# Regrouping a local unit's four feed-forward output runs in a two-layer transformer kernel

## The chip, the core and the metric

The kernel runs on one core of one Trainium2 chip, as one launch. The metric is the time of one execution on the device, in microseconds, as the median of several executions. A profiled execution gives, beside its own time, a span from its first to its last instruction and a trace of every engine: TensorE (PE, with its weight loads as PEld), VectorE (DVE), ScalarE (ACT), GpSimd (POOL) and SyncE (SP, which here only issues DMAs).

## The reference, cut to what matters

```python
x = L0_attn_X                                            # 8 sequences x 512 tokens x 256
x = x + L0_attn(layernorm(x));  x = x + L0_experts(layernorm(x))
x = x + L1_attn(layernorm(x));  x = x + L1_local(layernorm(x))

def L1_local(x):                                         # two layers of this:
    for l in range(2):
        q, k, v = split(shift_token(x) @ wqkv[l])        # 8 heads of 64
        q, k = rotary_xpos(l2norm(q) * qs[l], l2norm(k) * ks[l])
        o = softmax over the own and the previous window of 128 tokens
        x = x + o @ wo[l]
        h = layernorm(shift_token(x)) * lg[l] + lb[l]
        a, g = split(h @ w1[l] + b1[l])                  # 682 wide each
        x = x + (a * gelu(g)) @ w2[l] + b2[l]
    return x
```

The change concerns the last line of the local layers, `(a * gelu(g)) @ w2 + b2`, and the q and k columns of `h @ wqkv` of the unit that comes after. Everything is float32.

## The kernel before, in words

The program runs four stages: attention, the experts (up to 575 us), attention of 16 heads (597 to 1174 us), and the local layers (to the end, 2553 us, their first products lying among the last work of the stage before). A local **unit** is one layer of one sequence of 512 tokens; there are 16 units, in four blocks of 128 tokens each (`t` = 0 to 3).

The loop at L1581 is a pipeline written out by hand. Iteration n works on four units at once: `u` = unit n (attention, block by block), `ahead` = unit n+1 (its projections, later its rotations), `late` = unit n-1 (its norm and the first feed-forward product, "gated"), and `last` = unit n-2 (the second feed-forward product, "back"). The attention of block t is emitted in the order `flip_weights(t)` (the transposes `pt`), `outputs(t)` (`ov`), `scores(t+1)` (`sc`), `exponentials(t+1)`, `project(t)` (`pr`), `weigh(t+1)`. The table `fill` says what of the three other units stands between: `fill[t][0]` between the transposes and `ov`, `fill[t][1]` between `ov` and the scores, `fill[t][2]` after `pr`. The `weigh` of a quad of heads is emitted after the first and after the second step of `fill[t][2]`.

What the steps around the change do:

- `back(t)` (L1102): 6 float32 products of 256 columns, which the trace shows as 12 matmuls `fo`; five have 128 rows of weights, the last has 43 (42 hidden rows and the bias). VectorE then adds the result to the residual (L1122).
- `rows(t, s)` (L865), s = 0 for q and 1 for k: the products `qp` (4 matmuls of 512 columns), ScalarE's square `sq` (L870), VectorE's products with the rotary tables (L872, and L877 twice) and the sum of squares (L886), GpSimd's sum (L885).
- `flip()` (L840): the transposes `tp` of the next unit's rows, copied by ScalarE (L851).
- `norm()` (L1025): statistics (L1030 to L1032), the root on ScalarE (L114), then eight VectorE instructions that write `hn` (L1039). Half of a normed row is the row of the token before; for this `project(t)` (L1005) sends the rows through two DMAs into `late` (L1021, L1023) after its sum (L1018).
- `flip_normed()` (L1048): the transposes `tp` of `hn`, and VectorE's scale and shift into `hT`, a half at a time (L1058). `gated(i)` (L1067), the next consumer, multiplies with both halves of `hT` (`fp`).
- `masked_largest` (L148, called at L934): eight VectorE instructions on the scores of a block, which ScalarE's eight exponentials wait for.

What sets the order. Every product and every transpose of these stages goes through `product` and `transpose` (L161, L165), which pin it behind the instruction traced before it on its engine, so TensorE's order is the code's. So are ScalarE's exponentials, table loads and roots: a root is pinned behind the ScalarE instruction emitted just before it. The other instructions of VectorE, ScalarE and GpSimd are ordered by the framework's planner at build time, from its own estimates of when their inputs are ready. At run time each engine's queue keeps that order.

All of `fo`, `qp`, `tp`, `tpq` and `fp` take their PSUM tile from the pool `ps` (L1130), which has three slots, in turn. `pt` and `sc` share two slots of `psb`; `ov` and `pr` share the one of `psa`.

Of the kernel before, what the change touches and what calls it, by code (L numbers as in the profile page):

```python
# [53 lines left out]
def forward_kernel(  # L54
# [140 lines left out]
    with ExitStack() as st:  # L195
# [289 lines left out]
        for b in range(B):  # L485
            keep = tc.keep_in_program_order
            for t in range(NT):
# [9 lines left out]
                last = (b, t - 1) if t else (b - 1, NT - 1)  # L497
# [45 lines left out]
    with ExitStack() as st:  # L543
# [8 lines left out]
        number, steps = slots[0:1, :NS], slots[:, NS : NS + 32]  # L552
# [160 lines left out]
        ahead = None  # L713
        for s in range(NS):
# [4 lines left out]
            ahead = (s, hT, g, c2, r)  # L719
# [22 lines left out]
    def load_qkv(l, pool):  # L742
        wqkv = pool.tile([P, NC, 3 * INNER], F32, name=f"wqkv2_{l}")
        later(nc.sync.dma_start(out=wqkv, in_=wqkv2[l].rearrange("(c p) o -> p c o", p=P)))
        return wqkv

    def load_layer(l):
        wo = wl.tile([P, INNER // P, D], F32, tag="wo2", name=f"wo2_{l}")
        later(nc.sync.dma_start(out=wo, in_=wo2[l].rearrange("(c p) o -> p c o", p=P)))
        wf1 = wl.tile([P, NC, 2 * FULL + GATE + LAST], F32, tag="wf1", name=f"wf1_{l}")  # L750
        later(nc.sync.dma_start(out=wf1, in_=w1[l].rearrange("(c p) o -> p c o", p=P)))

        wf2 = wl.tile([P, NFC, D], F32, tag="wf2", name=f"wf2_{l}")
        for dst, src in (
            (wf2[:, : NFC - 1, :], w2[l, :FULL, :].rearrange("(c p) o -> p c o", p=P)),
            (wf2[:LAST, NFC - 1, :], w2[l, FULL:, :]),
            (wf2[LAST : LAST + 1, NFC - 1, :], b2[l : l + 1, :]),
        ):
            later(nc.sync.dma_start(out=dst, in_=src))
        return wo, wf1, wf2  # L760
# [375 lines left out]
    with ExitStack() as st:  # L1136
# [379 lines left out]
        for slot in range(max(max(fill) + 1, END + 3)):  # L1516
            steps = []
# [25 lines left out]
    with ExitStack() as st:  # L1543
        d1 = st.enter_context(tc.tile_pool(name="pD1", bufs=1))
        d2 = st.enter_context(tc.tile_pool(name="pD2", bufs=2))
        psb = st.enter_context(tc.tile_pool(name="psDb", bufs=2, space=PSUM))
        psa = st.enter_context(tc.tile_pool(name="psDa", bufs=1, space=PSUM))

        wqkv_of.append(load_qkv(1, d1))

        uT = d1.tile([P, NFC, L], F32, name="uT")
        nc.vector.memset(uT[:, NFC - 1, :], 1.0)
        lates = [d1.tile([P, NT, P], F32, name=f"late{i}") for i in range(2)]
        for late in lates:
            nc.gpsimd.memset(late[0:1, 0, :], 0.0)

        qT = d1.tile([P, H2 // 2, L], F32, name="qT")
        kT = d1.tile([P, H2 // 2, L], F32, name="kT")

        def unit(n):  # L1560
            return units[n] if 0 <= n < len(units) else None

        def steps(u, *names):

            return [(getattr(u, name), args) for name, *args in names] if u else []

        u = units[0]
        for t in range(NT):
            u.turn(t)
            if t == 0:  # L1570
                for quad in range(2):
                    u.scores(0, quad)
                for quad in range(2):
                    u.exponentials(0, quad)
        for quad in range(2):
            u.weigh(0, quad)

        for n in range(len(units) + 2):  # L1581
            u, ahead, late, last = unit(n), unit(n + 1), unit(n - 1), unit(n - 2)
            fill = [
                [
                    steps(last, ("back", 0)),
                    steps(late, ("norm",)) + steps(last, ("back", 1)) + steps(ahead, ("flip",)),
                    steps(last, ("back", 2))
                    + steps(ahead, ("rows", 0, 0))
                    + steps(last, ("back", 3))
                    + steps(ahead, ("rows", 0, 1))  # L1590
                    + steps(late, ("flip_normed",)),
                ],
                [
                    steps(late, ("gated", 0), ("gated", 1)),
                    steps(ahead, ("value_rows", 0)),
                    steps(ahead, ("rows", 1, 0), ("rows", 1, 1), ("rows", 2, 0)),
                ],
                [
                    steps(late, ("gated", 2), ("gated", 3)),
                    [],  # L1600
                    steps(ahead, ("rows", 2, 1), ("rows", 3, 0), ("rows", 3, 1)),
                ],
                [
                    steps(ahead, ("roots",)) + steps(late, ("gated", 4), ("gated", 5)),
                    steps(ahead, *(("turn", t) for t in range(NT))),
                    steps(ahead, *(("value_rows", t) for t in range(1, NT))),
                ],
            ]
            for t in range(NT):
                then, at = (u, t + 1) if t + 1 < NT else (ahead, 0)  # L1610
                if u:
                    u.flip_weights(t)
                for do, args in fill[t][0]:
                    do(*args)
                if u:
                    u.outputs(t)
                for do, args in fill[t][1]:
                    do(*args)
                if then:
                    for quad in range(2):  # L1620
                        then.scores(at, quad)
                    for quad in range(2):
                        then.exponentials(at, quad)
                if u:
                    u.project(t)
                rest = fill[t][2]
                for i, (do, args) in enumerate(rest):
                    do(*args)
                    if i < 2 and then:
                        then.weigh(at, i)  # L1630
                if then:
                    for i in range(len(rest), 2):
                        then.weigh(at, i)
            if u and u.b == B - 1 and u.l + 1 < DEPTH:
                layers.append(load_layer(u.l + 1))
# [146 lines left out]
```

## Time and profile before

| | |
|---|---|
| runs (3) | median 2559.63 us, 2558.3 to 2562.59 |
| the profiled execution | 2554.89 us, of which its span is 2553.2 us |
| granted TensorE clock | 0.987 over the span; 1.00 in the local layers |
| 0 to 560 us | PE busy 518.09, DVE 253.83, ACT 116.25 |
| 560 to 1240 us | PE busy 628.27, DVE 449.58, ACT 319.23 |
| 1240 us to the end | PE busy 1293.15, DVE 847.03, ACT 686.98, POOL 162.22 |
| one iteration of the loop (1413.37 to 1498.88 us) | 85.51 us: PE busy 85.18, DVE 56.93, ACT 45.97, POOL 10.21 |

The iterations that have all four units (n = 2 to 14, 13 of them) begin 85.50 to 85.52 us apart, so one iteration can be read for all. Times below that are given "in the iteration" count from the start of its first `pt` run, which in the one shown is at 1413.37 us. A run is a stretch of TensorE matmuls of one kind; in a row of the timeline the second number is the time from the first start to the modelled end of the last, and the difference between the starts of two rows is what a run really takes up.

### The profile page before, as it was taken

The page shows a single profiled execution, that of the slowest core. Times are in us where ns is not written, and L with a number is a line of the kernel's source. Part 1 is how long each engine was busy: PE and PEld are TensorE (multiplying, and loading weights), DVE is VectorE, ACT ScalarE, POOL GpSimd, SP SyncE. Part 2 cuts the span into 40 slices and gives each one's busy share as a digit, 9 for nine tenths or more (in the row PEclk, how much of TensorE's full clock was granted, in tenths as well). Part 3 has the DMA queues.
Part 4 walks back from the last instruction along what each step waited for, and adds up shares of the span by engine and source line. Part 5 has one row for each costly group of instructions (what it writes and reads, how often), then busy time and mean ns, then how long its engine had stood idle before and what let it go on. Part 6 is the DMA issues. An engine that isn't in the chain of part 4 may idle for free.

```text
span 2553.2 us, 39603 instructions
## 1 busy us (share of the span) xinstructions
PE 2439.5 (96%) x14374; PEld 1560.1 (61%) x14374; DVE 1550.4 (61%) x4739; ACT 1122.5 (44%) x2504; POOL 471.0 (18%) x642
## 2 busy tenths in 40 slices
PE   8998699996999999998899999999999999999998
PEld 5666588883455555445566666666666666666565
DVE  6775322224667777666667566756676667666653
ACT  2222121112455555545465455555555555555552
POOL 2232101003333332231111011100111111111100
PEclk9999899997999999999999999999999999999999
DMA  5340666631012000001000000000000000000000
GB/s 172 102 144 34 202 230 229 206 132 54 9 35 74 14 12 12 9 11 52 4 4 4 4 4 4 4 4 4 12 8 33 20 4 21 20 21 4 20 21 27
DMA packets 79030, 126.45 MB, mean 50 GB/s; under 512 B 13406, under 2 KB 56820, under 8 KB 78580
## 3 DMA queue, kind: packets, MB, share of 16 engines
q1 hardware_dynamic: 73236, 109.37, 12.9%
q0 software_dynamic: 4096, 12.59, 1.4%
q8 instruction: 115, 1.88, 0.3%
q10 hardware_dynamic: 1504, 1.97, 0.2%
q14 instruction: 79, 0.65, 0.1%
HBM read 97.82 MB, written 29.10 MB: 50 GB/s over the span
## 4 chain that ended last, share of the span: by engine, by line
PE 67%; DVE 6%; ACT 2%; DMA 1%; issue 1%; POOL 0%; SPq 0%; DVEq 0%; POOLq 0%; ACTq 0%
PE qp L163 12%; PE fp L163 12%; PE fo L163 7%; PE sc L163 7%; PE ov L163 7%; PE sd L163 5%; PE pr L163 5%; PE tpq L166 4%; PE pt L166 3%; PE qk L163 2%; DVE scrap L150 1%; PE tp L166 1%; PE vp L163 1%; DVE hT L1058 1%; DVE turn L877 1%; ACT prob L944 1%
## 5 line engine op out<-in xcount | busy, mean ns | idle before, releaser
L885 POOL TENSOR_TENSOR turned<-turned,turn 128x512 f32<-128x512 f32 x128 | 163.4, 1276 | 1060.1 <-DVE turn L877 1019.4
L163 PE MATMUL qp<-wqkv,xT 128*128 128x512 f32 x768 | 350.7, 598 | 0.0
L150 DVE CUSTOM_DVE_ANT_0 scrap<-sc,masks 128x256 f32<-128x256 f32 (+1 forms) x500 | 243.1, 486 | 134.3 <-PE sc L163 118.7
L163 PE MATMUL fp<-hT,wf 128*128 128x512 f32 (+1 forms) x704 | 313.5, 595 | 5.8 <-DVE hT L1058 5.7
L163 PE MATMUL sc<-kT,qT 64*128 64x256 f32 (+2 forms) x2024 | 305.3, 420 | 9.4 <-DVE qrow L150 7.7
L150 DVE CUSTOM_DVE_ANT_0 prob<-sc,masks 128x256 f32<-128x256 f32 (+1 forms) x512 | 164.4, 387 | 147.9 <-PE sc L163 147.9
L1326 ACT ACTIVATE pT<-sd 128x768 f32<-128x768 f32 (+1 forms) x192 | 169.3, 882 | 182.8 <-PE sc L163 92.6
L944 ACT ACTIVATE prob<-prob,nmax 128x256 f32<-128x256 f32 (+1 forms) x512 | 239.1, 468 | 22.5 <-DVE nmax L150 21.9
L163 PEld LDWEIGHTS qp<-wqkv,xT 128*128 128x128 f32 x768 | 141.6, 190 | 152.1 <-issue 134.4
L163 PEld LDWEIGHTS fp<-hT,wf 128*128 128x128 f32 (+1 forms) x704 | 127.9, 188 | 158.3 <-issue 138.9
L163 PE MATMUL sd<-qA,kT 32*128 32x512 f32 (+3 forms) x1024 | 194.4, 474 | 11.1 <-ACT pT L1326 9.0
L163 PEld LDWEIGHTS sc<-kT,qT 32*128 32x128 f32 (+1 forms) x2024 | 167.8, 187 | 59.3 <-DVE qrow L150 27.8
L163 PE MATMUL fo<-wf,uT 128*128 128x256 f32 (+1 forms) x768 | 190.4, 390 | 0.0
L690 DVE TENSOR_SCALAR hT<-hp,c 128x128 f32<-128x128 f32 x156 | 54.4, 349 | 211.7 <-ACT hT L688 211.7
L688 ACT ACTIVATE hT<-hp,c 128x128 f32<-128x128 f32 x156 | 57.4, 368 | 259.6 <-PE hp L678 221.3
L163 PEld LDWEIGHTS fo<-wf,uT 128*128 128x128 f32 (+1 forms) x768 | 137.6, 189 | 46.7 <-issue 29.6
L678 PEld LDWEIGHTS hp<-gT,we 128*128 128x128 f32 x1248 | 148.3, 193 | 26.1 <-DVE hT L690 14.1
L678 PE MATMUL hp<-gT,we 128*128 128x128 f32 x1248 | 159.8, 282 | 3.3 <-DVE krow L1164 1.6
L870 ACT ACTIVATE sq<-qp 128x512 f32<-128x512 f32 x128 | 75.8, 593 | 178.7 <-PE qp L163 135.7
L701 PE MATMUL yp<-w_all,hT 128*128 x624 | 153.7, 380 | 0.6 <-ACT hT L688 0.6
L1328 POOL TENSOR_SCALAR_AFFINE_SELECT pT<-pT 128x256 f32<-128x256 f32 x256 | 101.8, 411 | 277.8 <-ACT pT L1326 277.7
L1098 DVE SCALAR_TENSOR_TENSOR uT<-fp,b_sb,ge 128x512 f32<-128x512 f32 x96 | 69.9, 740 | 124.0 <-PE fp L163 119.2
(223 smaller groups left out, 4098.5 us busy)
## 6 DMA issues: line engine op xcount, KB each, us to landing
we<-in_ew SPq DMA_DIRECT2D x39, 1024.0 KB
g<-rows_in SPq DMA_DIRECT2D x39, 256.0 KB
w_all<-in_ew SPq DMA_DIRECT2D x8, 1024.0 KB
rows_out<-in_c_zero SPq DMA_DIRECT2D x3, 1664.0 KB
c<-in_eb SPq DMA_DIRECT2D x39, 128.0 KB
rows_out<-y SPq DMA_DIRECT2D x39, 128.0 KB
xb<-in_x_in SPq DMA_DIRECT2D x8, 512.0 KB
kept<-x SPq DMA_DIRECT2D x8, 512.0 KB
```

What stands on the lines that cost most here:

```text
L150: nc.vector.tensor_tensor_reduce(out=out, in0=scores, in1=mask, scale=-1.0, scalar=-MASKED, op0=ALU.add, op1=ALU.min, accum_out=largest,)
L163: tc.keep_in_program_order(nc.tensor.matmul(*args, **kw))
L166: tc.keep_in_program_order(nc.tensor.transpose(dst, src, ident))
L678: nc.tensor.matmul(hp[:, f, :], we[:, c, f * P : (f + 1) * P], gT[:, c, :], start=(c == 0), stop=(c == NC - 1),)
L688: nc.scalar.activation(hT[:, f, :], hp[:, f, :], AF.Relu, bias=bias)
L701: nc.tensor.matmul(yp, hT[:, f, :], w2_all[:, bass.ds(e, 1), f * D : (f + 1) * D].rearrange("p a d -> p (a d)"), start=(f == 0), stop=(f = ...
L870: nc.scalar.activation(sq, qp, AF.Square)
L885: nc.gpsimd.tensor_tensor(own.turned[:, t, s], own.turned[:, t, s], turn, ALU.add)
L944: nc.scalar.activation(pr[:, j, lo:], pr[:, j, lo:], AF.Exp, scale=-1.0, bias=nmax[:, j : j + 1], accum_out=sums[:, j : j + 1],)
L1098: nc.vector.scalar_tensor_tensor(uT[:n, i, :], val[:n, :], b1_sb[:n, l, 0, i : i + 1], ge[:n, :], ALU.add, ALU.mult)
L1326: nc.scalar.activation(pT[:, :, :at], sc[:, :, :at], AF.Exp)
L1328: nc.gpsimd.affine_select(out=pT[:, :, a : a + P], in_=pT[:, :, a : a + P], compare_op=ALU.is_ge, fill=0.0, base=0, pattern=[[0, 2], [1, P ...
```

## The change

The list `fill[0]` is rewritten. All steps are kept; only their order within block 0 changes, and with it the order in which everything of theirs is emitted.

```diff
             fill = [
                 [
-                    steps(last, ("back", 0)),
-                    steps(late, ("norm",)) + steps(last, ("back", 1)) + steps(ahead, ("flip",)),
-                    steps(last, ("back", 2))
-                    + steps(ahead, ("rows", 0, 0))
-                    + steps(last, ("back", 3))
-                    + steps(ahead, ("rows", 0, 1))
+                    steps(last, ("back", 0), ("back", 1)),
+                    steps(late, ("norm",)) + steps(ahead, ("flip",)),
+                    steps(last, ("back", 2), ("back", 3))
+                    + steps(ahead, ("rows", 0, 0), ("rows", 0, 1))
                     + steps(late, ("flip_normed",)),
                 ],
```

On TensorE, block 0 before: `pt`, back 0, `ov`, back 1, `tp` (flip), `sc`, `pr`, back 2, rows 0 q, back 3, rows 0 k, `tp` (normed). After: `pt`, back 0, back 1, `ov`, `tp` (flip), `sc`, `pr`, back 2, back 3, rows 0 q, rows 0 k, `tp` (normed). The `weigh` of the first quad is still emitted behind back 2; that of the second stands behind back 3 instead of behind rows 0 q.

## The prediction

> **What bounds the kernel.** I read the page first, then the waits from 1327.86 us on (the iterations with all four units), then TensorE's and VectorE's timelines of one iteration, then the end of the trace. The page says who fills the span:
>
> ```profile
> span 2553.2 us, 39603 instructions
> PE 2439.5 (96%) x14374; PEld 1560.1 (61%) x14374; DVE 1550.4 (61%) x4739; ACT 1122.5 (44%) x2504; POOL 471.0 (18%) x642
> PEclk9999899997999999999999999999999999999999
> ```
>
> TensorE is full, and in the local layers at a granted clock of 1.00. An iteration is 85.51 us with PE busy 85.18, so the change can act in two ways only: on what TensorE's own runs take up, and on the few places where it waits. VectorE's long waits there are these:
>
> ```profile
> DVE uT L1098 <- PE fp L163: 101.7, 43, 3.1
> DVE st L1031 <- DMA late<-x: 99.6, 31, 4.0
> ```
>
> The second is in play: an instruction of the norm's statistics waits in VectorE's queue for a DMA, with others behind it. TensorE in block 0:
>
> ```profile
> 1414.24 2.95 PE L163 MATMUL fo<-wf,uT 128*128 128x256 f32 x12
> 1417.12 1.09 PE L163 MATMUL ov<-pT,v 128*64 128x128 f32 x16
> 1418.15 3.05 PE L163 MATMUL fo<-wf,uT 128*128 128x256 f32 x12
> 1421.13 1.09 PE L166 MATMUL tp<-ident,x 128*128 128x128 f32 x8
> ...
> 1428.79 1.98 PE L163 MATMUL qp<-wqkv,xT 128*128 128x512 f32 x4
> 1430.61 2.95 PE L163 MATMUL fo<-wf,uT 128*128 128x256 f32 x12
> 1433.49 1.98 PE L163 MATMUL qp<-wqkv,xT 128*128 128x512 f32 x4
> 1435.31 1.14 PE L166 MATMUL tp<-ident,hn 128*128 128x128 f32 x8
> ...
> 1438.03 1.02 PE L163 MATMUL fp<-hT,wf 128*128 128x512 f32 x2
> 1439.38 1.13 PE L163 MATMUL fp<-hT,wf 128*128 128x512 f32 x2 [0.33 <-DVE hT L1058]
> ```
>
> The one wait is the last row: the second half of `fp` starts 1.35 us after the first, where two such matmuls take 0.86, and restarts 0.10 slow (534 ns to the next start instead of 429). That is 0.60 us here, 0.62 us on average over the 13 iterations, 8.0 us in all: the most that the change can gain in waits. VectorE says why `hT` is late:
>
> ```profile
> 1429.28 0.42 DVE L1122 TENSOR_TENSOR x<-fo,x 128x256 f32<-128x256 f32 x1
> 1433.06 0.29 DVE L1031 BATCH_NORM_STATS2 st<-late 128x6 f32<-128x128 f32 x1 [3.37 <-DMA late<-x]
> ...
> 1433.51 0.64 DVE L872 TENSOR_TENSOR turned<-qp,tab 128x512 f32<-128x512 f32 x1
> ...
> 1435.95 0.81 DVE L1058 TENSOR_SCALAR hT<-tp,lng_sb,lnb_sb 128x512 f32<-128x512 f32 x1 [0.22 <-PE tp L166]
> 1436.68 0.68 DVE L872 TENSOR_TENSOR turned<-qp,tab 128x512 f32<-128x512 f32 x1
> ...
> 1438.53 0.80 DVE L1058 TENSOR_SCALAR hT<-tp,lng_sb,lnb_sb 128x512 f32<-128x512 f32 x1
> ```
>
> The q rows (first L872) are held until the DMA lands, and the k rows stand between the two halves of `hT`.
>
> **Part 1: TensorE's runs.** A `fo` run takes 2.88 us to the next start: 12 x 0.216, plus 0.093 and 0.104 where it goes from 128 to 43 rows of weights, plus 0.09 where it leaves 43 rows again. The next run then opens slowly: `qp` 533 ns instead of 429, `ov` +50, `tp` +59; `fo` behind `ov` 320 instead of 216. TensorEngine Tiling (the Trainium skill, Key Properties) says that changing the tiling mode drains TensorE. Counted by boundaries of kinds, nine become six, and at 0.15 to 0.2 us each this would be 0.5 us an iteration, 6 us gained. Counted as the rule is worded, by mode, nothing is saved: each `fo` run ends in another mode than it begins in, so `fo` to `fo` is a change as well. The trace decides this: at the end of the kernel four `back` runs stand together,
>
> ```profile
> 2536.68 11.89 PE L163 MATMUL fo<-wf,uT 128*128 128x256 f32 x48
> ```
>
> and 11.89 us is no less than 4 x 2.95; at each seam a start-to-start time of 306 is followed by one of 320. So: removed, `fo` to `ov` (0.14), `ov` to `fo` (0.20), `fo` to `tp` (0.15), twice `fo` to `qp` (0.19 each); added, twice `fo` to `fo` (0.19 each), `fo` to `ov` (0.14), `ov` to `tp` (0.155, taken from `ov` to `tpq`), `fo` to `qp` (0.19). 0.87 against 0.87. I take 0; bounds -0.01 to +0.01 us an iteration. In the iteration, `sc` still starts at 8.78, `pr` at 10.71, `tp` (normed) at 21.94; moved are `ov` (its run ends at 7.75 instead of 4.77), back 3 (ends at 18.40 instead of 20.12) and the q rows (end at 20.22 instead of 17.24).
>
> **Part 2: what hangs on `ov`.** The root of the norm is pinned behind ScalarE's copy of `ov`; the eight `hn` (pitch 0.257) began 1.18 us after `ov` ended, and will run from 8.93 to 10.99. The maxima of the scores, queued behind them, began at 9.97, so they slip by 1.02, and the exponentials with them (last one ends at 15.5 instead of 14.48). Cover: the weighted scores are needed at 22.9 (`pt`), now ready about 17.3 instead of 16.0; the copy of `ov` is needed at 10.71 and ends at 8.45. These cost 0. What has little cover is L1018, the sum of `pr`, because the DMA into `late` follows it. Before, it ran behind the weighing of quad 0, at 14.07, and the DMA landed at 19.7. If it keeps that place it slips to 15.1 and the landing to 20.7. Its input, though, was ready at 12.65, 0.07 before the reciprocal that went ahead; with the maxima 1.02 later it should come first, at 13.75, and the landing is then near 19.4. I take 19.4 and keep 20.7 for the range.
>
> **Part 3: the q rows.** They are in PSUM at 20.22. L872 waits for the square (its recorded wait is for ScalarE): square from 20.42 to 21.02, q rows from 21.05 instead of 20.14. So the DMA wait that held them is hidden, and yet they start 0.9 us later, because their product was moved by 2.98. Back 3's sum (0.7 with its wait, at 21.95 before) leaves the stretch behind them; it is done before. The q rows (1.84) end at 22.89. The k rows' square ends at 22.74, so both the k rows and the first `hT` (ready at 22.58) stand ready. The k rows come earlier in the code: I expect them first. K rows 22.89 to 24.75, `hT` from 24.75 and 25.47. TensorE restarts 0.85 behind the start of an `hT` (1438.53 to 1439.38), so `fp` begins at 25.60 instead of 24.66, slowly (0.10), and its second half at 26.56 with no wait, where it was 26.01 with 0.10 after it: +0.45 us an iteration. If the first `hT` keeps its place ahead of the k rows, the second starts at 25.47 instead of 25.16: +0.31. The PSUM slots move too: the second normed `tp` takes the q rows' slot (free at 22.35, needed at 22.38) instead of back 3's, where it lost about 0.1; nothing is gained, for `hT` ends later. What follows `fp` has no slack on TensorE, so 13 x 0.45 = 5.9 us; with the other order 13 x 0.31 = 4.0.
>
> Outside the 13 iterations: n = 0 and 1 have no `back`, n = 15 has no rows, n = 16 and 17 only shuffle VectorE's sums. 0. The sum for the profiled execution: its 2554.9 us, 1.7 of it outside the span, becomes 2560.8. The same 5.9 on the median of 2559.63, which lies 4.7 above that execution, gives 2565.5.
>
> **The rivals.**
> 1. *The late fetch also bites* (30%). L1018 keeps its place, the landing is at 20.7, the statistics take 0.45 and back 3's sum 0.35 behind it, so the q rows start at 21.5: +0.76 (first `hT` ahead of the k rows) to +0.90 us, 2569.5 to 2571.3. For it: in the trace the weighing goes ahead of this sum in blocks 1 and 2 too. Against it: the ready times above.
> 2. *The sums of squares give way* (14%); not slower. Nothing needs L886 before the roots of block 3, 0.6 us each. If the planner puts the k rows' one behind the second `hT`, that starts at 24.9, before the 25.16 which is the point from which it decides: -0.29, 2555.8. With both behind, nothing is left of the wait: down to -0.62 x 13, 2551.6. Against it: in every iteration L886 directly follows its L877.
> 3. *The change does nothing that TensorE sees* (11%): VectorE's order falls so that the second half of `fp` starts at 26.0 as before, within 0.1 us an iteration, 2558.3 to 2560.9. For it: two shifts of about 0.9 us against each other. Against it: q rows, k rows and one `hT` are 4.4 us of VectorE work behind 21.05, and only leaving some of it for later helps.
>
> **The numbers.** My forecast, +0.31 to +0.45, has 45%. About 0.2% (5.1 us) is what a measurement of this kernel tells from no change; the forecast straddles it: 26 of the 45 above, 19 below. Slower by more: 26 + 30 = 56%. Within: 19 + 11 + 6 (the mild half of rival 2) = 36%. Faster: 8%. The range leaves out the strong half of rival 2 and little at the top: 2555.5 to 2573, the forecast's own 2563.6 to 2565.5.
>
> **What would show it.** TensorE's `fo` rows become x24, each near 5.8 us, with `tp` (normed) still 21.94 after `pt`: part 1. `hn` from about 8.9, the maxima from about 11.0: part 2. VectorE's wait on `late` ending before the q rows' square ends: the forecast; after: rival 1. The row `fp` with a wait of about 1.0 us on its first matmul (k rows ahead) or more than 0.33 on its third (`hT` ahead), and iterations of 85.8 to 86.0 us: part 3. Iterations of 85.2 or less, with L886 behind L1058: rival 2. I am wrong altogether if `fo` to `fo` costs less than 0.1, or if the time changes outside block 0.

## The result and the profile after

| | before | after |
|---|---|---|
| median, 20 runs each | 2561.78 us (2558.06 to 2563.84) | 2566.88 us (2564.12 to 2570.64) |
| ratio, after to before | | 1.0023 (95% interval 1.0016 to 1.0029) |
| one iteration, mean of 13 | 85.51 us | 85.98 us |

The changed kernel is slower by 0.23%, which is 5.9 us of 2561.78 (4.1 to 7.4 by the interval; the two medians lie 5.1 apart); 13 iterations of +0.474 us are 6.2 us. The iteration is the better measure: its 13 lengths lie between 85.504 and 85.517 us before and between 85.980 and 85.987 after, while whole runs of one kernel spread over 6 us.

The page after, its first two lines, says little:

```profile
span 2567.5 us, 39604 instructions
PE 2448.0 (95%) x14374; PEld 1565.2 (61%) x14374; DVE 1550.3 (60%) x4739; ACT 1119.2 (44%) x2504; POOL 470.7 (18%) x642
```

Its span is 14.3 us longer, but only 6.2 of that is in the 13 iterations; 7.2 had gathered before the first of them began (1335.07 us instead of 1327.86), in code that the change doesn't touch: 4.4 before the loop, and 2.8 in its iteration n = 0, which took 67.41 us at a mean granted clock of 0.95 in the trace of before and 70.24 us at 0.90 here. The profiled execution took 2569.18 us, near the top of its kernel's runs. TensorE's timeline of one iteration (start, length, instruction; this one begins at 1421.06 us) answers part 1:

```profile
1421.93 5.93 PE L163 MATMUL fo<-wf,uT 128*128 128x256 f32 x24
1427.80 1.09 PE L163 MATMUL ov<-pT,v 128*64 128x128 f32 x16
1428.82 1.09 PE L166 MATMUL tp<-ident,x 128*128 128x128 f32 x8
...
1433.60 5.93 PE L163 MATMUL fo<-wf,uT 128*128 128x256 f32 x24
1439.46 3.70 PE L163 MATMUL qp<-wqkv,xT 128*128 128x512 f32 x8
1443.00 1.24 PE L166 MATMUL tp<-ident,hn 128*128 128x128 f32 x8
1444.08 1.91 PE L166 MATMUL pt<-ident,prob 128*128 128x128 f32 x16
1446.68 3.70 PE L163 MATMUL fp<-hT,wf 128*128 128x512 f32 x8 [0.70 <-DVE hT L1058]
```

Four runs of `fo` are two of 24, and the normed `tp` starts at 1443.00 - 1421.06 = 21.94 us into the iteration, exactly where it did before. What is new is in the last row: `fp` now waits on its first matmul, for `hT`, and not at all on its third, where the wait was before. VectorE over the same time:

```profile
1440.72 0.29 DVE L1031 BATCH_NORM_STATS2 st<-late 128x6 f32<-128x128 f32 x1 [2.03 <-DMA late<-x]
1441.05 0.21 DVE L1032 BATCH_NORM_AGGREGATE mv<-st 128x2 f32<-128x12 f32 x1
1441.18 0.37 DVE L1122 TENSOR_TENSOR x<-fo,x 128x256 f32<-128x256 f32 x1
1442.11 0.69 DVE L872 TENSOR_TENSOR turned<-qp,tab 128x512 f32<-128x512 f32 x1 [0.56 <-ACT sq L870]
1442.72 0.75 DVE L877 TENSOR_TENSOR turn<-qp,tab 128x256 f32<-128x256 f32 x2
1443.38 0.68 DVE L886 TENSOR_REDUCE ss<-sq 128x8 f32<-128x512 f32 x1
1443.97 0.68 DVE L872 TENSOR_TENSOR turned<-qp,tab 128x512 f32<-128x512 f32 x1
...
1445.82 1.52 DVE L1058 TENSOR_SCALAR hT<-tp,lng_sb,lnb_sb 128x512 f32<-128x512 f32 x2
```

The DMA's landing still ends a wait (first row), but 1.4 us before the q rows could start. What holds the q rows is the square on ScalarE (fourth row). From there to the `hT` row VectorE has no gap: q rows 21.05, k rows 22.91, `hT` 24.76 us into the iteration.

### The profile page after: what moved, and what is told of

Its sections match the earlier page's. It is cut to its first block, busy times and chain, and to the rows that moved or that the text cites. A ratio compares the mean times of both kernels' runs of the same rounds, so it can differ in the third digit from the quotient of the medians.

```text
span 2567.5 us, 39604 instructions
## 1 busy us (share of the span) xinstructions
PE 2448.0 (95%) x14374; PEld 1565.2 (61%) x14374; DVE 1550.3 (60%) x4739; ACT 1119.2 (44%) x2504; POOL 470.7 (18%) x642
## 4 chain that ended last, share of the span: by engine, by line
PE 66%; DVE 7%; ACT 2%; DMA 1%; issue 1%; POOL 0%; SPq 0%; DVEq 0%; POOLq 0%; ACTq 0%
PE fp L163 12%; PE qp L163 11%; PE fo L163 7%; PE ov L163 7%; PE sc L163 7%; PE sd L163 5%; PE pr L163 5%; PE tpq L166 4%; PE pt L166 2%; PE qk L163 2%; DVE scrap L150 1%; DVE turn L877 1%; PE tp L166 1%; DVE ss L886 1%; DVE turned L872 1%; PE vp L163 1%
## 5 line engine op out<-in xcount | busy, mean ns | idle before, releaser
L1098 DVE SCALAR_TENSOR_TENSOR uT<-fp,b_sb,ge 128x512 f32<-128x512 f32 x96 | 69.9, 741 | 125.7 <-PE fp L163 121.0
```

What stands on the lines that cost most here:

```text
L1098: nc.vector.scalar_tensor_tensor(uT[:n, i, :], val[:n, :], b1_sb[:n, l, 0, i : i + 1], ge[:n, :], ALU.add, ALU.mult)
```

## The experiments

No kernel here leaves out or changes any of the computation. The experiments ran on three chips, 5 to 20 executions of each kernel, beside executions of the kernel before on the same chip; its median was 2560.1, 2572.9 and 2574.7 us on the three, so the ratio and the iteration (the mean of 13 in the trace) are given.

| run | order of block 0 behind `pr`, or edit | iteration, us | ratio to before (95%) |
|---|---|---|---|
| before | back 2, q, back 3, k, `tp` | 85.51 | 1 |
| after | back 2, back 3, q, k, `tp` | 85.98 | 1.0023 (1.0016 to 1.0029) |
| e1_first_pair | as before; only backs 0, 1 paired | 85.51 | 0.9998 (0.9989 to 1.0007) |
| e2_second_pair | as after; only backs 2, 3 paired | 85.98 | 1.0027 (1.0018 to 1.0035) |
| e3_sum_behind | as after, k sum behind `tp` | 85.38 | 0.9999 (0.9990 to 1.0008) |
| e5_q_first | q, back 2, back 3, k, `tp` | 85.51 | 0.9998 (0.9984 to 1.0012) |
| e6_qk_first | q, k, back 2, back 3, `tp` | 84.76 | 0.9963 (0.9950 to 0.9976) |
| e8_singles_rows_first | q, back 2, k, back 3, `tp` | 84.76 | 0.9969 (0.9957 to 0.9981) |
| e4_k_behind | back 2, back 3, q, `tp`, k | 85.55 | 1.0002 (0.9989 to 1.0015) |
| e7_before_k_behind | back 2, q, back 3, `tp`, k | 86.23 (mean of 12) | 1.0032 (1.0021 to 1.0043) |
| e9_square_after | as after, squares behind the products | 86.11 | 1.0040 (1.0025 to 1.0056) |

Of `e7_before_k_behind` one iteration of 87.95 us is left out, because the granted clock dipped in it (last section). Of `e9_square_after` twelve iterations lie at 86.08 or 86.09 and one, at a clock of 1.00, at 86.37.

**Each pair by itself.** `e1_first_pair` takes the changed lines for the first half and those of before for the second; `e2_second_pair` the other way round.

```diff
 # e1_first_pair, against the kernel before
-                    steps(last, ("back", 0)),
-                    steps(late, ("norm",)) + steps(last, ("back", 1)) + steps(ahead, ("flip",)),
+                    steps(last, ("back", 0), ("back", 1)),
+                    steps(late, ("norm",)) + steps(ahead, ("flip",)),
 # e2_second_pair, against the kernel before
-                    steps(last, ("back", 2))
-                    + steps(ahead, ("rows", 0, 0))
-                    + steps(last, ("back", 3))
-                    + steps(ahead, ("rows", 0, 1))
+                    steps(last, ("back", 2), ("back", 3))
+                    + steps(ahead, ("rows", 0, 0), ("rows", 0, 1))
```

> Only back 0 and back 1 are joined ahead of ov; back 2, q rows, back 3, k rows stand as in the kernel before. Theory (the loss is VectorE's work behind the q rows, which the second pair moves): ov ends at 7.75 and hn slips to about 9.2 as in the changed kernel, but the second half of fp starts at 26.0 as before, and an iteration is 85.5 us (+-0.05); time as before within 1 us. Rival 'first pair' (a seam of two runs, or the slip of hn, maxima and the late fetch, is what costs): 85.7 us or more, +3 us or more.

> Only back 2 and back 3 are joined, the q and k rows together behind them; the first half of block 0 stands as in the kernel before. Theory: q rows on VectorE from 21.05, k rows straight behind them, first hT about 24.8, fp from 25.6, an iteration of 85.98 us (+-0.05), +6 us: the whole loss of the change. Rival 'first pair': 85.75 us or less, the rest of the loss being that of the half that is not here.

Measured: 85.506 and 85.976 us. The first pair delays `ov` by 3 us and `hn` to 9.27, and costs nothing; the second is the whole loss. The wait in `e1_first_pair` is that of the kernel before, on the third matmul of `fp`:

```profile
1444.24 1.02 PE L163 MATMUL fp<-hT,wf 128*128 128x512 f32 x2
1445.56 1.56 PE L163 MATMUL fp<-hT,wf 128*128 128x512 f32 x3 [0.30 <-DVE hT L1058]
```

The rival "first pair" is out.

**0.6 us of VectorE work taken from ahead of `hT`.** The sum of squares becomes a step of its own:

```diff
-            nc.vector.tensor_reduce(self.ss[:, t, s, :], sq, AX.X, ALU.add)
+            self.sq = sq
+            if not later:
+                self.sums(t, s)
+        def sums(self, t, s):
+            nc.vector.tensor_reduce(self.ss[:, t, s, :], self.sq, AX.X, ALU.add)
...
-                    + steps(ahead, ("rows", 0, 0), ("rows", 0, 1))
-                    + steps(late, ("flip_normed",)),
+                    + steps(ahead, ("rows", 0, 0), ("rows", 0, 1, True))
+                    + steps(late, ("flip_normed",))
+                    + steps(ahead, ("sums", 0, 1)),
```

> The changed kernel, with the k rows' sum of squares (0.6 us of VectorE) emitted behind the normed transposes instead of ahead of them; all else the same. Theory: each half of hT starts 0.6 us earlier, fp from 25.0 instead of 25.62, an iteration of 85.98 - 0.60 = 85.38 us, which is 0.13 us below the kernel before: about -1.7 us against it. Rival 'late fetch' (the queue is held by the DMA, not by this work): 85.98 us unchanged. Rival 'first pair': unchanged too.

Measured: 85.383, to 3 ns what was expected. VectorE's rows show the swap, `hT` (L1063 here) ahead of the sum (L891):

```profile
1441.95 0.75 DVE L877 TENSOR_TENSOR turn<-qp,tab 128x256 f32<-128x256 f32 x2
1442.61 1.52 DVE L1063 TENSOR_SCALAR hT<-tp,lng_sb,lnb_sb 128x512 f32<-128x512 f32 x2
1444.05 0.67 DVE L891 TENSOR_REDUCE ss<-sq 128x8 f32<-128x512 f32 x1
```

Taking 0.60 us out from ahead of `hT` takes 0.60 us off the iteration, with the DMA where it was. So VectorE's work there, and not the late fetch, is what TensorE waits for. The whole-time comparison alone (0.9999) couldn't have said it.

**The q rows or the k rows?**

```diff
 # e5_q_first, against the changed kernel
-                    steps(last, ("back", 2), ("back", 3))
-                    + steps(ahead, ("rows", 0, 0), ("rows", 0, 1))
+                    steps(ahead, ("rows", 0, 0))
+                    + steps(last, ("back", 2), ("back", 3))
+                    + steps(ahead, ("rows", 0, 1))
 # e6_qk_first: both rows ahead of the backs
+                    steps(ahead, ("rows", 0, 0), ("rows", 0, 1))
+                    + steps(last, ("back", 2), ("back", 3))
```

> The pairs stay, and of the next unit's rows only the q rows stand ahead of back 2; the k rows stay behind back 3. Theory: the q rows cost nothing any more, but the k rows still reach PSUM at 21.9, their square ends at 22.7 when the first hT is ready already (22.6), so VectorE runs first hT, k rows, second hT as in the kernel before, and the second half of fp starts at 26.0: 85.51 us an iteration (+-0.1), time as before. Rival 'the q rows' hold by the late fetch made the wait of the kernel before': with the q rows done by 19.1 the wait is gone, 84.9 us and -8 us.

> The pairs stay pairs, but the q and k rows of the next unit stand ahead of back 2 and back 3 instead of behind them; same instructions. Theory: VectorE turns both rows while TensorE is in the 5.9 us of the two backs, both halves of hT follow their transposes at once (22.6 and 23.3), fp starts at 24.6 with no wait, and the iteration loses the wait that the kernel before had too: 85.51 - 0.62 = 84.9 us, -8 us against the kernel before, -14 against the changed one. Rival 'late fetch': the q and k rows are held on VectorE behind the DMA to 19.7 or more, back 3 waits for the q rows' PSUM slot, 85.5 us or more. Rival 'first pair': 85.98, since that half is unchanged.

With the q rows early the iteration is that of the kernel before, 85.511, though VectorE sits idle for 1.9 us just before the first `hT`:

```profile
1450.88 0.81 DVE L1058 TENSOR_SCALAR hT<-tp,lng_sb,lnb_sb 128x512 f32<-128x512 f32 x1 [1.93 <-PE tp L166]
1451.60 0.68 DVE L872 TENSOR_TENSOR turned<-qp,tab 128x512 f32<-128x512 f32 x1
...
1453.45 0.81 DVE L1058 TENSOR_SCALAR hT<-tp,lng_sb,lnb_sb 128x512 f32<-128x512 f32 x1
```

The k rows still stand between the halves, and that alone makes the wait. With both rows early, 84.761 us: `hT` follows its transposes, and TensorE's timeline has no wait left in block 0:

```profile
1431.93 3.60 PE L163 MATMUL qp<-wqkv,xT 128*128 128x512 f32 x8
1435.37 5.93 PE L163 MATMUL fo<-wf,uT 128*128 128x256 f32 x24
1441.23 1.09 PE L166 MATMUL tp<-ident,hn 128*128 128x128 f32 x8
1442.15 1.91 PE L166 MATMUL pt<-ident,prob 128*128 128x128 f32 x16
1443.90 2.31 PE L163 MATMUL fp<-hT,wf 128*128 128x512 f32 x5
```

This beats both kernels, by 0.37% the one before. It is 0.14 below the 84.9 expected: the normed `tp` loses no time at its fifth transpose any more (about 0.1 before), and a seam (the place where one run follows another) of `fo` to `qp` has become one of `fo` to `tp` (0.19 to 0.15).

**Pairs or singles?**

```diff
 # e8_singles_rows_first, against the kernel before
-                    steps(last, ("back", 2))
-                    + steps(ahead, ("rows", 0, 0))
-                    + steps(last, ("back", 3))
-                    + steps(ahead, ("rows", 0, 1))
+                    steps(ahead, ("rows", 0, 0))
+                    + steps(last, ("back", 2))
+                    + steps(ahead, ("rows", 0, 1))
+                    + steps(last, ("back", 3))
```

> Four single backs as in the kernel before, but the q rows stand ahead of back 2 and the k rows ahead of back 3. Theory (whether the backs stand singly or in pairs is worth nothing; where the k rows stand is worth all): the k rows are off VectorE by 22.0, both hT follow their transposes, 84.8 us an iteration (+-0.1), -9 us against the kernel before, as the version with pairs and both rows first (84.76). Rival 'the pairing itself helps once the wait is gone': 85.0 us or more.

84.764 against 84.761 with pairs. Four single runs or two pairs make 3 ns; where the k rows stand makes 0.75 us (`e5_q_first` against `e6_qk_first`), and one back of 2.9 us between them and the normed `tp` is enough for it.

**The k rows behind the transposes.** `e4_k_behind` edits the changed kernel, `e7_before_k_behind` the one before, in the same way:

```diff
-                    + steps(ahead, ("rows", 0, 1))
-                    + steps(late, ("flip_normed",)),
+                    + steps(late, ("flip_normed",))
+                    + steps(ahead, ("rows", 0, 1)),
```

> The changed kernel, with the k rows behind the normed transposes, so that nothing stands ahead of hT but the q rows. Theory by VectorE alone: no wait of fp, 84.9 us an iteration. Theory with the three PSUM slots: the k rows' product takes the q rows' slot, which VectorE frees only at about 22.8, since it takes the first hT ahead of the q rows; TensorE stops 1.7 us ahead of the k rows' product, and an iteration is 86.6 us (+-0.15), +14 us against the kernel before.

> The kernel before, with the k rows behind the normed transposes. Theory by VectorE alone: the k rows no longer stand between the halves of hT, 84.9 us an iteration. Theory with the three PSUM slots: the second normed transpose takes the q rows' slot, which is held while the q rows wait on VectorE behind the late fetch (to 21.4), so TensorE stops about 0.9 us there; 85.75 us (+-0.15), +3 us: the place where the late fetch does reach TensorE.

Both expectations missed. TensorE in `e4_k_behind`, and then in `e7_before_k_behind`:

```profile
1453.40 1.04 PE L166 MATMUL tp<-ident,hn 128*128 128x128 f32 x8
1454.90 1.98 PE L163 MATMUL qp<-wqkv,xT 128*128 128x512 f32 x4 [0.47 <-DVE hT L1058]
```

```profile
1453.32 0.66 PE L166 MATMUL tp<-ident,hn 128*128 128x128 f32 x4
1454.80 0.63 PE L166 MATMUL tp<-ident,hn 128*128 128x128 f32 x4 [0.82 <-DVE turn L877]
1455.63 1.98 PE L163 MATMUL qp<-wqkv,xT 128*128 128x512 f32 x4 [0.20 <-DVE x L1122]
```

In the first, the k rows' product waits for the first `hT`, that is for the slot of the first normed `tp`, and not for the q rows' slot as I had it. VectorE was still reading the q rows then, to 1456.11 us:

```profile
1455.36 0.75 DVE L877 TENSOR_TENSOR turn<-qp,tab 128x256 f32<-128x256 f32 x2
```

So here the three slots of `ps` don't go round in turn; why the planner took another one no run shows. 0.63 us lost instead of 1.7.

In the second, the wait of 0.82 us for the q rows' slot is the one I expected; the second wait, for back 3's sum, which had queued up behind the q rows, I had missed. (In turn, the k rows do take back 3's slot.) Here the late fetch does reach TensorE, since it holds the q rows that hold the slot:

```profile
1452.90 0.29 DVE L1031 BATCH_NORM_STATS2 st<-late 128x6 f32<-128x128 f32 x1 [3.37 <-DMA late<-x]
...
1453.35 0.64 DVE L872 TENSOR_TENSOR turned<-qp,tab 128x512 f32<-128x512 f32 x1
```

The iterations themselves confirm it. In this kernel the wait for the DMA ends 19.60 to 19.72 us into the iteration, and the iterations are 86.16 to 86.28 us long, one for one: their length less the end of the wait is 66.55 or 66.56 us in all twelve. In the kernel before, the same wait ends at 19.61 to 19.73, and the iterations differ by no more than 0.013 us.

Neither kernel waits for `hT` at `fp` any more; in both the PSUM slots give most of the gain back, or more.

**The square.** In all rows, the square is emitted behind the products:

```diff
-            sq = own.pool.tile(shape, F32, tag="sq", name="sq", bufs=2)
-            nc.scalar.activation(sq, qp, AF.Square)
...
+            sq = own.pool.tile(shape, F32, tag="sq", name="sq", bufs=2)
+            nc.scalar.activation(sq, qp, AF.Square)
             nc.gpsimd.tensor_tensor(own.turned[:, t, s], own.turned[:, t, s], turn, ALU.add)
```

> The changed kernel, with the square of every q and k row emitted behind VectorE's three products of that row instead of ahead of them, so that the square waits for the products and no longer the products for the square. Theory: in block 0 the q rows start on VectorE at about 20.35 instead of 21.05 and the k rows at about 22.05 instead of 22.9; by the order that the planner gives now (q products, first k product, q sum, k products, first hT, k sum, second hT) the first hT starts near 23.9 and the second near 25.2, TensorE's first fp starts on time (24.7) and the third about 26.05: an iteration of 85.5 us (+-0.1), the loss of the change taken back without moving anything on TensorE. Rival (the start at 21.05 came from something else, such as the late fetch or back 3's sum, which end at 20.5): q rows still at 21.0 or more, 85.9 us or more.

Half a hit. The first k product now waits for TensorE alone, and the q product starts 0.63 us earlier (20.42 into the iteration):

```profile
1454.00 0.69 DVE L870 TENSOR_TENSOR turned<-qp,tab 128x512 f32<-128x512 f32 x1
...
1455.72 0.69 DVE L870 TENSOR_TENSOR turned<-qp,tab 128x512 f32<-128x512 f32 x1 [0.36 <-PE qp L163]
```

So the square did set the 21.05. But block 0 wins 0.22 us instead of 0.5, since the second `hT` starts at 25.41 and not 25.2: the k rows' sum ahead of it has to wait for their square, which now ends at 24.78. And the order of all other rows changed as well: the transposes `tpq` of block 3 take 4.41 us instead of 4.10, and the iteration is longer than 85.98.

```profile
1503.87 0.19 DVE L896 TENSOR_SCALAR ss<-ss 128x64 f32<-128x64 f32 x1
...
1507.18 4.48 PE L166 MATMUL tpq<-ident,turned 128*128 128x128 f32 x32
1511.60 1.16 PE L163 MATMUL sc<-kT,qT 64*128 64x128 f32 x16
```

VectorE's chain ahead of these transposes (L896, L904, L1098) starts 70.29 us into the iteration, where it was 70.20 in the changed kernel; TensorE comes to them 0.21 us earlier (73.60 instead of 73.81) and leaves them 0.10 later (78.02 instead of 77.91). That VectorE holds them there is read from the two traces and was not tested by a run of its own.

## Why the prediction was right, point by point

- **TensorE's runs: right.** Taken as 0; the normed `tp` is at 21.94 in both traces. The seams inside the new runs show 305 or 306 ns and then 320, as at the kernel's end. `e6_qk_first` and `e8_singles_rows_first`, 3 ns apart, show that regrouping by itself is worth nothing. The rule that a change of tiling mode drains TensorE (the Trainium skill, TensorEngine Tiling (Array Packing), Key Properties) gives this answer if 43 rows of weights count as another mode than 128. The page doesn't say so; the traces fit it, since `sc` to `pr`, from 64 rows to 128, shows the same 305 and then 320 ns.
- **What hangs on `ov`: right in effect, off in size.** `hn` starts at 9.27, not 8.93, because a copy of `flip` (L851) went between the two activations of the root, and the maxima at 11.33, not 10.99. L1018 did go ahead of the reciprocal, but at 14.08, not 13.75, and the DMA landed at 19.66, not 19.4. All of it is covered, as `e1_first_pair` shows. With that, rival 1 fell.
- **The q rows: right.** 21.05, then k rows 22.91 (22.89 expected), `hT` 24.76 (24.75), `fp` 25.62 (25.60). +0.474 us an iteration instead of +0.45: 6.2 us instead of 5.9. Whether the whole time moved by more than the prediction's 0.2% stays open: 0.16 to 0.29% by the interval.
- **Rival 2** named a lever: moving one sum of squares is worth 0.60 us an iteration in `e3_sum_behind`, and the order that it needs did not come by itself.
- **Wrong in the reading of before:** I put the held q rows (the DMA) beside the k rows as what makes `hT` late. `e5_q_first` takes the first away and the wait stays, to 2 ns. The row of the first `hT` had said it already: VectorE stood idle for 0.22 us ahead of it, waiting for TensorE's transposes. The long wait of 3.37 us in VectorE's queue cost TensorE nothing there.
- **Wrong about PSUM, though not in the forecast:** the slots were taken as going round in turn. The waits of the changed kernel fit that: the second normed `tp` goes on at 22.55 us, 0.15 us after VectorE's last instruction on the q rows (L877) ended, and it does so in `e7_before_k_behind` too. That cost 0.2 us where I had none to 0.1, without harm, since `fp` was waiting anyway. In `e4_k_behind` the rule itself failed and put the expectation off by 1.1 us.

## What to carry to other kernels

When a queue of one engine is full, ask of a moved step not what it costs there but what its consumers have to do, and how soon behind it somebody needs them: the k rows were 1.7 us of TensorE wherever they stood, but their 1.9 us of VectorE work is free ahead of a 2.9 us run of something else and cost 0.6 us just ahead of the transposes. A wait that is long in the waits' list is not for that a cause; take it away and look. And where a loop repeats, measure its period in the trace: here it tells 5 ns, where whole runs hardly tell 3 us.

## What the runs showed of the hardware that was not expected

The granted clock dips at places and in sizes that change from execution to execution. The iteration n = 0, which the change leaves as it was, shows it (the column behind POOL's is the granted clock); first the trace of before, then of after:

```profile
1182.65:1250.06 67.41, 56.57 (x355) 39.46 (x354) 48.47 (x143) 34.33 (x97) 10.16 (x8) 0.95 0.03 11
1187.05:1257.29 70.24, 59.32 (x355) 41.43 (x353) 48.48 (x143) 34.30 (x97) 10.16 (x8) 0.90 0.03 10
```

The tail of the program behind the last full iteration took 113.7 us in the trace of before and 120.6 in that of `e1_first_pair`, and the windows of the latter show why:

```profile
2464.60:2483.60 19.00, 15.58 (x94) 9.87 (x93) 11.45 (x31) 9.58 (x22) 2.35 (x1) 0.97 0.16 57
2483.60:2502.60 19.00, 17.21 (x88) 10.47 (x86) 7.72 (x27) 9.58 (x22) 0.00 (x0) 0.85 0.01 2
2502.60:2521.60 19.00, 17.37 (x80) 11.17 (x79) 5.23 (x9) 5.53 (x6) 0.00 (x0) 0.82 0.03 7
```

In the trace of before this stretch has a clock of 1.00. Such dips are as large as the change studied, which is why the iterations, at a clock of 1.00, carry the verdicts here. One iteration of the eleven traces had a dip of its own, in `e7_before_k_behind`; its neighbours took 86.27 and 86.28 us:

```profile
1778.10:1866.05 87.95, 86.92 (x453) 54.62 (x452) 56.94 (x162) 45.95 (x110) 10.20 (x8) 0.98 0.03 8
```
